# Layer 2's experts in a four-layer hybrid: gate logits moved into the attention's steps, networks computed four at a time

## The chip, the core and the metric

The program runs on one core of one Trainium2 chip, in one launch. Its time is device microseconds (us) of that core; the kernel before has a median of 11329.03 us over 3 runs (11311.37 to 11329.67).

The engines are TensorE (PE; its weight loads are listed as PEld), VectorE (DVE), ScalarE (ACT), GpSimd (POOL) and SyncE (SP). Every transfer in this program is issued on SP, in the order of one queue. All arithmetic is in 32-bit floats.

## The reference, cut to what matters

Four layers work on x of shape 4 x 64 x 64 x 128 (4 images, 4096 tokens of 128 channels). Layer 2 is an attention followed by the experts that the change touches:

```
t = t + attention(ln(t))
t = t + experts(ln(t))

def experts(x):                                    # x: 4 images x 4096 tokens x 128
    logits = einsum('bsd,ed->bse', x, gate_w) + gate_b      # 64 experts
    probs  = softmax(logits, axis=1)                        # over the 4096 tokens
    topv, topi = the 8 highest of each image and expert
    pooled = sum over the 8 of topv * x[topi]               # 4 x 64 x 128
    h   = gelu([pooled, 1] @ weight1)                       # 129 -> 512, one network an expert
    out = [h, 1] @ weight2                                  # 513 -> 128
    each of the 8 tokens gets topv * out added
```

The weights are 64 networks of 129 x 512 and 513 x 128 floats, some 33.7 MB, and each network is applied to just 4 vectors (one an image).

## The kernel before, in words

The layers run one after another. Layers 0 and 1 and layer 2's attention are interleaved in hand-written generators; `experts` and the start of `layer3` are plain code whose order on each engine is chosen by a planner (it keeps the order of the code unless an instruction would have to wait for something longer than a later one).

**The attention** (`recurrence_and_attention`) walks a list `seq` of 4 images x 8 query blocks of 512 tokens x 16 steps (512 steps). A step issues, in this order, the scores of the step two ahead (`scores(g + 2)`: two matmuls L1351 and their exponentials L1355), a second exponential (L1394), and the two matmuls of its own pair of key tiles into `avs` (L1399). The order on PE, ACT and DVE is exactly the order of the code there (`manual_schedule`); SP and POOL are ordered by the planner. Between these, two generators are advanced: `own` prepares the next image (`prepare`, with `unit` for layer 1's recurrence; several advances a step, none while the last image is worked on), and `side`, advanced once a step, does the block's small work: `finish` of the block before (normalise, add the residual in the tile `tb`, store it to `xa` at L1319) and `query` of the block after. A `yield` in a generator is the place where it hands back to the step. `finish` and `query` share one PSUM bank, `blk`.

**The experts** (`experts`) then load all of `xa` into a resident tile `t` (32 transfers, L2059). Images are taken in pairs, one image's 64 experts on partitions 0 to 63 and the other's on 64 to 127. For a pair: layer norm into `xl` (L135, L137, L85, L142), transposes (L103), logits (L1449, evacuated by ACT at L1450) into `wt`; softmax and the choice of the 8 highest over 4096 columns (L1455 to L1465, one long instruction each); transposes of the weights (L103) and the pooled sums (L1476), with the tokens as the stationary operand.

The networks follow, two experts a turn (`EG = 2`). The *weights* are the stationary operand: 8 matmuls of 128 x 128 with a moving operand of 4 columns for the first layer (L1502), bias (L1507), Gelu (L1512), 8 more for the second (L1516). A 32-bit matmul is two records in the trace, so a turn has 16 records of each. The weights are loaded in a ring of 3 (L1490, L1495). At the end the outputs are laid out as `oute` (L1525, L1529), and for each of 32 blocks 4 matmuls (L1537) form the scattered sum, which DVE adds to `t` (L1542) and SP stores to `x2` (L1543). Layer 3 loads `x2` again (L1659).

Buffers come from stacked pools. A pool that lies where an earlier one lay starts only when every tile of the earlier one has been released.

Of the kernel before, what the change touches and what calls it, by code (L numbers as in the profile page):

```python
# [14 lines left out]
P = 128  # L15
B = 4
# [27 lines left out]
EG = 2  # L44
# [834 lines left out]
def recurrence_and_attention(cm, x1, W, V, sp_d, x2, last):  # L879
# [7 lines left out]
    with ExitStack() as ctx:  # L887
# [17 lines left out]
        nc.vector.memset(qrow[:, P - 1 : P], -0.5)  # L905
        with tc.tile_pool(name="rwp", bufs=2) as lp, tc.tile_pool(
# [30 lines left out]
            nc.vector.tensor_copy(wv[:, D : D + 1], cm.ident[:, P - 1 : P])  # L937

# [357 lines left out]
        def finish(b, k):  # L1296
# [23 lines left out]
            yield  # L1320

# [16 lines left out]

        NP = NT // 2
        seq = [(b, k, p) for b in range(B) for k in range(NBLK) for p in range(NP)]  # L1340
        avs, res, es = {}, {}, {}
# [23 lines left out]
        with tc.manual_schedule(engines=engines):  # L1365
# [4 lines left out]
            for g, (b, k, p) in enumerate(seq):  # L1370
                if k == 0 and p == 0:
                    own = prepare(b + 1, own_bank) if b + 1 < B else iter(())
                if p == 0:
                    gens = []
                    if g:
                        gens.append(finish(*seq[g - 1][0:2]))
                    if k + 1 < NBLK:
                        gens.append(query(b, k + 1, block_bank))
                    side = steps(*gens)
                    tb = tl(p2, [P, 4, D], "tb")  # L1380
                    nc.sync.dma_start(tb, rows(img[b]["t"], 0, k))
                    res[b, k] = tb
                    avs[b, k] = tl(avp, [P, BLK], "av")
                if p == NP - 3:
                    for _ in side:
                        pass
                    if k == NBLK - 1:
                        for _ in own:
                            pass
# [16 lines left out]
            for _ in finish(*seq[-1][0:2]):  # L1406
                pass
# [3 lines left out]
def experts(cm, W, t, x2):  # L1411
    tc, nc = cm.tc, cm.nc
    with ExitStack() as ctx:
        wp = ctx.enter_context(tc.tile_pool(name="xw", bufs=1))
        wl = ctx.enter_context(tc.tile_pool(name="xwl", bufs=3))
        mm = ctx.enter_context(tc.tile_pool(name="xmm", bufs=6, space=PSUM))
        acc = ctx.enter_context(tc.tile_pool(name="xacc", bufs=2, space=PSUM))

        gwT = tl(wp, [P, E2], "gwT")
        b1T = tl(wp, [P, H2 // P, E2], "b1T")  # L1420
        with tc.tile_pool(name="xwp", bufs=2) as lp:
            cm.load_transposed(gwT, W["gate_w"], lp, mm, "mm")
            for c in range(H2 // P):
                cm.load_transposed(
                    b1T[:, c, :], W["weight1"][:, D, c * P : (c + 1) * P], lp, mm, "mm"
                )
        gb = tl(wp, [P, 1], "gb")
        b2 = tl(wp, [P, D], "b2")
        with nc.allow_non_contiguous_dma(reason="a bias laid over partitions"):
            for i in range(2):  # L1430
                half = slice(i * E2, (i + 1) * E2)
                nc.sync.dma_start(gb[half, :], W["gate_b"].unsqueeze(1))
                nc.sync.dma_start(b2[half, :], W["weight2"][:, H2, :])
# [3 lines left out]
        pooled = tl(wp, [P, E2, B], "pooled")  # L1437
        with tc.tile_pool(name="xb", bufs=1) as bp, tc.tile_pool(name="x2", bufs=2) as p2:
            for pr in range(2):
                xl = tl(bp, [P, 2, NT, D], "xl")  # L1440
                lg = wt[:, pr, :]
                for i in range(2):
                    cm.layer_norm(xl[:, i], t[:, 2 * pr + i], p2)
                    half = slice(i * E2, (i + 1) * E2)
                    for k in range(NBLK):
                        xT = tl(p2, [P, BLK], "xT")
                        cm.transpose4(xT, xl[:, i, 4 * k : 4 * k + 4, :], mm, "mm", act=False)
                        ps = tl(mm, [P, BLK], "mm")
                        nc.tensor.matmul(ps[half, :], lhsT=gwT, rhs=xT, start=True, stop=True)  # L1449
                        nc.scalar.activation(  # L1450
                            lg[half, k * BLK : (k + 1) * BLK], ps[half, :], AF.Identity,
                            bias=gb[half, :],
                        )
# [12 lines left out]
                wT = tl(bp, [P, NT, P], "wT")  # L1466
                for k in range(NBLK):
                    cm.transpose4(
                        wT[:, 4 * k : 4 * k + 4, :].rearrange("p a c -> p (a c)"),
                        lg[:, k * BLK : (k + 1) * BLK].rearrange("p (a c) -> p a c", c=P),  # L1470
                        mm, "mm", act=(k % 2 == 0),
                    )
                for i in range(2):
                    ps = tl(acc, [P, BLK], "acc")
                    for k in range(NT):
                        nc.tensor.matmul(  # L1476
                            ps[:, 0:E2], lhsT=xl[:, i, k, :],
                            rhs=wT[:, k, i * E2 : (i + 1) * E2],
                            start=(k == 0), stop=(k == NT - 1),
                        )  # L1480
                    nc.vector.tensor_copy(pooled[:, :, 2 * pr + i], ps[:, 0:E2])


        NC2 = H2 // P
        outT = tl(wp, [P, B, E2], "outT")
        oute = tl(wp, [P, 2, D], "oute")
        with tc.tile_pool(name="xh", bufs=3) as hp:
            for e0 in range(0, E2, EG):
                w1 = tl(wl, [P, EG, H2], "w1")
                nc.sync.dma_start(  # L1490
                    w1, W["weight1"][e0 : e0 + EG, 0:D, :].rearrange("e d h -> d e h")
                )
                w2 = tl(wl, [P, EG, NC2, D], "w2")
                for j in range(EG):
                    nc.sync.dma_start(  # L1495
                        w2[:, j],
                        W["weight2"][e0 + j, 0:H2, :].rearrange("(c p) o -> p c o", p=P),
                    )
                ph = tl(mm, [P, NC2, EG, B], "mm")
                for j in range(EG):  # L1500
                    for c in range(NC2):
                        nc.tensor.matmul(  # L1502
                            ph[:, c, j, :], lhsT=w1[:, j, c * P : (c + 1) * P],
                            rhs=pooled[:, e0 + j, :], start=True, stop=True,
                        )
                hh = tl(hp, [P, NC2, EG, B], "hh")
                nc.vector.tensor_tensor(  # L1507
                    hh, ph,
                    b1T[:, :, e0 : e0 + EG].unsqueeze(3).to_broadcast([P, NC2, EG, B]),
                    ALU.add,  # L1510
                )
                nc.scalar.activation(hh, hh, AF.Gelu)  # L1512
                po = tl(acc, [P, EG, B], "acc")
                for j in range(EG):
                    for c in range(NC2):
                        nc.tensor.matmul(  # L1516
                            po[:, j, :], lhsT=w2[:, j, c, :], rhs=hh[:, c, j, :],
                            start=(c == 0), stop=(c == NC2 - 1),
                        )
                nc.vector.tensor_copy(  # L1520
                    outT[:, :, e0 : e0 + EG], po.rearrange("p e b -> p b e")
                )
        for pr in range(2):
            ps = tl(mm, [P, BLK], "mm")
            nc.tensor.transpose(  # L1525
                ps[:, 0:P], outT[:, 2 * pr : 2 * pr + 2, :].rearrange("p b e -> p (b e)"),
                cm.ident,
            )
            nc.vector.tensor_tensor(oute[:, pr, :], ps[:, 0:P], b2, ALU.add)  # L1529
# [594 lines left out]
```

## Time and profile before

| what | value |
|---|---|
| median of 3 runs (lowest, highest) | 11329.03 us (11311.37, 11329.67) |
| the profiled execution: time, span in the trace | 11343.32 us, 11341.5 us |
| mean granted TensorE clock | 0.881 |
| busy share of the span: PE, DVE, ACT, POOL | 85%, 68%, 46%, 48% |
| attention's steps: first and last L1351 or L1399 | 6793.2 to 8811.5 us |
| experts: from there to the issue of the last store to `x2` (L1543) | to 9349.98 us |
| layer 3's first products (L1716) | 9404.65 us |

The attention's steps and the experts are 2018 us and 538 us of the span. The page's shares are means over stages of very different kinds, so the views used below are cut to stretches of these two. A row of the table by stretch gives the stretch, its length, busy us and number of instructions of each engine, the granted clock, the mean busy share of the 16 DMA engines (this can pass 1) and GB/s. A row of the groups gives line, engine, operation, output and inputs, shape, count, busy us and mean ns of one, then the engine's idle time before such an instruction and who ended it.

### The profile page before, as it was taken

The numbers are of one execution on the slowest core, as the hardware profiler recorded it, in microseconds if no ns is written. First come the engines' busy times: TensorE is split into PE (matmuls) and PEld (weight loads), VectorE is DVE, ScalarE is ACT, GpSimd is POOL, SyncE is SP. The second block draws the span as 40 slices with busy tenths as digits, with TensorE's granted clock in tenths as the row PEclk, the third lists the DMA queues.
The fourth block names the chain that finished last, engine by engine and source line by source line (L and its number), as shares of the span: only waits on it lengthen the run. The fifth ranks groups of instructions, "written<-read, shape, count | busy, mean of one in ns | idle before, by whom it ended". The sixth has DMA issues, their size and how long they took to land. (4 is left out here: it accounts for less than half of the span.)

```text
span 11341.5 us, 163279 instructions
## 1 busy us (share of the span) xinstructions
PE 9650.1 (85%) x59692; PEld 4750.2 (42%) x59692; DVE 7675.5 (68%) x11366; ACT 5226.4 (46%) x13141; POOL 5433.6 (48%) x2629
## 2 busy tenths in 40 slices
PE   6889998889997899988899739999999598687685
PEld 2344443344443344433444324444444394444442
DVE  1898898888988889888999775354410413565563
ACT  6666444555445564445522127677766102132230
POOL 0788888888888888888899610000000000110110
PEclk7899999899998899998999869999999755688785
DMA  5334443334443344433333321110000141000100
GB/s 146 107 110 147 129 126 116 114 113 151 139 128 116 110 140 139 136 121 113 105 109 101 127 65 31 32 33 28 22 12 9 48 140 14 6 15 10 14 8 8
DMA packets 1338551, 946.41 MB, mean 83 GB/s; under 512 B 692421, under 2 KB 1159849, under 8 KB 1333657
## 3 DMA queue, kind: packets, MB, share of 16 engines
q1 hardware_dynamic: 1337752, 935.95, 27.5%
q8 instruction: 478, 7.83, 0.3%
q14 instruction: 321, 2.62, 0.1%
HBM read 633.46 MB, written 302.12 MB: 82 GB/s over the span
## 5 line engine op out<-in xcount | busy, mean ns | idle before, releaser
L657 DVE TENSOR_TENSOR_SCAN big<-dA,db 128x1024 f32<-128x1024 f32 x2048 | 4679.9, 2286 | 81.1 <-ACT dA L564 2.8
L673 POOL TENSOR_TENSOR big<-big,ct 128x2048 f32<-128x2048 f32 x1024 | 4646.5, 4538 | 85.5 <-DVE big L657 6.1
L641 PE MATMUL db<-dg,du 64*64 64x512 f32 x16384 | 2446.6, 618 | 100.6 <-DVE db L654 87.6
L686 PE MATMUL aux<-big,both 128*64 128x256 f32 x16384 | 2109.8, 401 | 471.6 <-DVE db L654 257.1
L686 PEld LDWEIGHTS aux<-big,both 128*64 128x64 f32 x16384 | 1203.2, 142 | 1466.0 <-issue 625.9
L705 ACT COPY yr<-aux 128x64 f32<-128x64 f32 x1024 | 226.2, 221 | 2758.8 <-PE aux L686 1315.2
L641 PEld LDWEIGHTS db<-dg,du 64*64 64x64 f32 x16384 | 747.7, 136 | 1323.7 <-issue 1220.5
L612 ACT ACTIVATE dg<-mask,BT 128x64 f32<-128x64 f32 x4096 | 1007.3, 341 | 5.9 <-DMA dg_d<-dg 5.9
L1399 PE MATMUL av<-e,x 128*128 128x512 f32 x2048 | 974.0, 592 | 5.9 <-ACT e L1394 5.9
L1351 PE MATMUL qk<-a,xT 128*128 128x512 f32 x2048 | 963.3, 593 | 9.8 <-ACT e L1355 9.0
L1355 ACT ACTIVATE e<-qk,nk 128x512 f32<-128x512 f32 x1024 | 692.3, 685 | 539.6 <-PE qk L1351 538.8
L564 ACT ACTIVATE dA<-dp,A 128x252 f32<-128x252 f32 x2048 | 870.6, 509 | 1.4
L1809 POOL COPY vp<-vt 72x160 f32<-72x160 f32 x56 | 19.0, 345 | 1389.9 <-PE po L1815 1082.0
L968 POOL TENSOR_TENSOR ln_rs<-ln_rs,qrow 128x8 f32<-128x8 f32 x16 | 26.2, 1640 | 1323.7 <-DVE ln_rs L967 1323.7
L665 POOL TENSOR_TENSOR cy<-big,a 128x32 f32<-128x32 f32 x1008 | 271.2, 269 | 742.5 <-DVE big L657 480.0
L1351 PEld LDWEIGHTS qk<-a,xT 128*128 128x128 f32 x2048 | 383.0, 190 | 467.9 <-issue 371.3
L1399 PEld LDWEIGHTS av<-e,x 128*128 128x128 f32 x2048 | 381.6, 190 | 436.1 <-issue 394.4
L2009 DVE SCALAR_TENSOR_TENSOR t<-x,gw,t 128x128 f32<-128x128 f32 x1024 | 354.2, 346 | 302.8 <-PE x L2003 279.8
L1394 ACT ACTIVATE e<-e 128x1024 f32<-128x1024 f32 x510 | 538.7, 1056 | 15.5
L1634 POOL MEMSET f<- 128x2016 f32 x1 | 1.8, 1778 | 1093.1 <-DMA t<-x 1093.1
L654 DVE TENSOR_TENSOR db<-db,cy 128x16 f32<-128x16 f32 x2016 | 336.2, 167 | 262.6 <-PE db L641 210.7
L1799 ACT ACTIVATE e<-s 72x576 f32<-72x576 f32 x448 | 269.8, 643 | 513.6 <-PE s L1792 513.1
(482 smaller groups left out, 11417.8 us busy)
## 6 DMA issues: line engine op xcount, KB each, us to landing
ct<-ct_d SPq DMA_DIRECT2D x1024, 128.0 KB
dg_d<-dg SPq DMA_DIRECT2D x256, 512.0 KB
dg<-dg_d SPq DMA_DIRECT2D x256, 512.0 KB
xo<-xT_d SPq DMA_DIRECT2D x2048, 32.0 KB
x<-xc_d SPq DMA_DIRECT2D x144, 264.0 KB
dp<-dl_d SPq DMA_DIRECT2D x256, 128.0 KB
t2k<-in_x SPq DMA_DIRECT2D x96, 256.0 KB
sp<-sp_d SPq DMA_DIRECT2D x16, 1280.0 KB
```

The costliest lines, as they stand in the source:

```text
L564: nc.scalar.activation(w["dA"][:, :, g, n, 1:], w["dp"][:, g, :, 1:], AF.Exp, scale=A[:, w["h"], g, n : n + 1],)
L612: nc.scalar.activation(q["dg"][:, n, :], mask, AF.Copy, scale=BT[:, q["c"], n : n + 1])
L641: nc.tensor.matmul(bs[j][p * TC : (p + 1) * TC, g * NH0 : (g + 1) * NH0, :], lhsT=q["du"][kp][half, g * TC : (g + 1) * TC], rhs=q["dg"][ha ...
L654: nc.vector.tensor_tensor(bs[j][:, :, 0], bs[j][:, :, 0], old[:, u, :], ALU.add)
L657: nc.vector.tensor_tensor_scan(st[:, u].rearrange("p n t -> p (n t)"), q["w"]["dA"][:, c % QC].rearrange("p g n t -> p (g n t)"), bs[j].re ...
L673: nc.gpsimd.tensor_tensor(sv, sv, q["ct"].rearrange("p n t -> p (n t)").unsqueeze(1) .to_broadcast([P, 4, NH0 * TC]), ALU.mult,)
L686: nc.tensor.matmul(yp[p * TC : (p + 1) * TC], lhsT=both, rhs=st[:, :, p * NH0 + n, :], start=(n == 0), stop=(n == NH0 - 1 and not late),)
L1351: nc.tensor.matmul(ps, lhsT=me["xT"][:, kt * P : (kt + 1) * P], rhs=me["a"][k], start=True, stop=True,)
L1355: nc.scalar.activation(e[:, j, :], ps, AF.Exp, bias=me["nk"][:, kt : kt + 1], scale=2.0)
L1394: nc.scalar.activation(es[g + 2], es[g + 2], AF.Exp)
L1399: nc.tensor.matmul(avs[b, k], lhsT=img[b]["x"][:, kt, :], rhs=e[:, j, :], start=(kt == 0), stop=(kt == NT - 1),)
L2009: nc.vector.scalar_tensor_tensor(t[:, j, :], s[:, e, :], gw[:, j, 4 * a + e : 4 * a + e + 1], t[:, j, :], ALU.mult, ALU.add,)
```

## The change

1. **Logits in the attention's steps.** A new generator `gate(b, k)` runs in `side`, behind `finish` and `query`: layer norm of the finished block `tb` (the root by POOL), a store of the normalised tokens `xh` to `xh_d`, four transposes, a copy, one matmul with `gwT`, bias by ACT, and a store of the logits to `lg_d`. The forced end of `side` moves from three steps before a block's end to the next block's start. Two small loads (`gb`) and one transposed load (`gwT`) move to the attention's set-up.
2. **No resident tokens.** `experts` loads the logits (two transfers of 2 MB) and, block by block, `xh` for the pooled sums and `xa` for the residual at the end (a ring of 6). The pooled sums have the tokens as the moving operand, on two halves of the columns.
3. **The networks.** Four experts a turn. `pooled` is widened from 4 to 32 columns by zeros. The *weights* move: four matmuls of 512 columns with 32 stationary columns, each on its own quarter of the columns, then bias and Gelu on a 128 x 512 tile, four transposes, and 16 matmuls of 128 moving columns, again on quarters. Biases of the first layer come as four loads of one row each, repeated over 32 partitions. The outputs go to DRAM in four small stores a turn and are read back as `oute`.
4. **Loads ahead.** The ring holds 5 turns (20 experts); its first 5 loads stand ahead of everything but the logits' loads.

```diff
-EG = 2
+EG = 4
 # recurrence_and_attention, set-up
+        gwT = tl(wp, [P, E2], "gwT")
+        gb = tl(wp, [P, 1], "gb")
...
+            cm.load_transposed(gwT, G["gate_w"], lp, pp, "mm")
+        def gate(b, k):
+            tb = done.pop((b, k))
...
+            for i in range(4):
+                nc.vector.bn_stats(st[:, i, :], tb[:, i, :])
+            for i in range(4):
+                nc.vector.bn_aggr(mv[:, i, :], st[:, i, :])
+            inverse_root(rs, mv[:, :, 1])
+            yield
+            yield
+            xh = tl(p3, [P, 4, D], "xh")
+            for i in range(4):
+                nc.vector.tensor_scalar(
+                    xh[:, i, :], tb[:, i, :], mv[:, i, 0:1], rs[:, i : i + 1],
+                    ALU.subtract, ALU.mult,
+                )
+            nc.sync.dma_start(rows(xh_d, b, k), xh)
+            yield
+            yield
+            ps = block_bank()
+            turned(ps, xh)
+            xhT = tl(p3, [P, BLK], "xhT")
+            nc.vector.tensor_copy(xhT, ps)
+            yield
+            yield
+            half = slice(b % 2 * E2, (b % 2 + 1) * E2)
+            ps = block_bank()
+            nc.tensor.matmul(ps[half, :], lhsT=gwT, rhs=xhT, start=True, stop=True)
+            lg = tl(p3, [P, BLK], "lg")
+            nc.scalar.activation(lg[half, :], ps[half, :], AF.Identity, bias=gb[half, :])
+            nc.sync.dma_start(lg_d[half, b // 2, k * BLK : (k + 1) * BLK], lg[half, :])
+            yield
 # the loop over the steps, at a block's first step
+                    for _ in side:
+                        pass
                     gens = []
                     if g:
                         gens.append(finish(*seq[g - 1][0:2]))
                     if k + 1 < NBLK:
                         gens.append(query(b, k + 1, block_bank))
+                    if g:
+                        gens.append(gate(*seq[g - 1][0:2]))
...
-            for _ in finish(*seq[-1][0:2]):
+            for _ in steps(finish(*seq[-1][0:2]), gate(*seq[-1][0:2])):
 # experts
+        wl = ctx.enter_context(tc.tile_pool(name="xwl", bufs=5))
         wp = ctx.enter_context(tc.tile_pool(name="xw", bufs=1))
-        wl = ctx.enter_context(tc.tile_pool(name="xwl", bufs=3))
...
+        for pr in range(2):
+            nc.sync.dma_start(wt[:, pr, :], lg_d[:, pr, :])
...
+        def weights(e0):
+            w1 = tl(wl, [P, EG, H2], "w1")
+            nc.sync.dma_start(
+                w1, W["weight1"][e0 : e0 + EG, 0:D, :].rearrange("e d h -> d e h")
+            )
...
+            for j in range(EG):
+                nc.sync.dma_start(
+                    w2[:, j], W["weight2"][e0 + j, 0:H2, :].rearrange("(c p) o -> p c o", p=P)
+                )
+                nc.sync.dma_start(
+                    b1[32 * j : 32 * j + 32, :],
+                    W["weight1"][e0 + j, D : D + 1, :].to_broadcast([32, H2]),
+                )
+            return w1, w2, b1
+        AHEAD = 5
+        ready = [weights(e0) for e0 in range(0, AHEAD * EG, EG)]
 # pooled sums, per pair and block
+                    for j in range(4):
+                        for i in range(2):
+                            half = slice(i * E2, (i + 1) * E2)
+                            nc.tensor.matmul(
+                                po[half, 0:D], lhsT=wT[:, j, half], rhs=xs[i][:, j, :],
+                                start=(4 * k + j == 0), stop=(4 * k + j == NT - 1),
+                            )
 # networks, per turn
+                w1, w2, b1 = ready.pop(0)
+                ph = tl(mm, [P, H2], "mm")
                 for j in range(EG):
+                    nc.tensor.matmul(
+                        ph[32 * j : 32 * j + 32, :], lhsT=pooled[:, e0 + j, :], rhs=w1[:, j, :],
+                        start=True, stop=True,
+                    )
...
+                nc.vector.tensor_tensor(flat, ph, b1, ALU.add)
+                nc.scalar.activation(flat, flat, AF.Gelu)
...
+                cm.transpose4(hT.rearrange("p c h -> p (c h)"), hh, mm, "mm", act=False)
...
+                for c in range(NC2):
+                    for j in range(EG):
+                        col = slice(32 * j, 32 * j + 32)
                         nc.tensor.matmul(
+                            po[col, 0:D], lhsT=hT[:, c, col], rhs=w2[:, j, c, :],
                             start=(c == 0), stop=(c == NC2 - 1),
                         )
...
+                if e0 + AHEAD * EG < E2:
+                    ready.append(weights(e0 + AHEAD * EG))
...
+                for b in range(B):
+                    nc.sync.dma_start(oe_d[b, e0 : e0 + EG, :], so[b::32, :])
```

## The prediction

> **What bounds the kernel now.** I read the page first for the span (11341.5 us, one execution of 11343.3; the runs shown have a median of 11329.0, so I sum a difference against the profiled execution and take it from the median). Then the busy times by stretch around the change:
>
> ```profile
> 8594.70:8811.80 217.10, 217.10 (x531) 97.97 (x529) 10.39 (x30) 145.41 (x181) 0.00 (x0) 1.00 0.03 9
> 8811.80:8856.20 44.40, 3.32 (x14) 1.87 (x13) 33.26 (x207) 1.93 (x3) 0.00 (x0) 0.54 0.93 235
> 8856.20:8908.80 52.60, 30.78 (x96) 11.26 (x96) 32.18 (x146) 11.45 (x18) 0.00 (x0) 0.81 0.11 31
> 8908.80:8933.30 24.50, 0.03 (x1) 0.06 (x1) 20.28 (x7) 5.09 (x4) 0.00 (x0) 0.54 0.00 0
> 8933.30:8953.80 20.50, 20.20 (x160) 20.06 (x160) 3.31 (x7) 2.34 (x4) 0.00 (x0) 0.89 0.00 1
> 8953.80:9056.50 102.70, 56.05 (x256) 32.52 (x256) 50.82 (x94) 18.36 (x23) 0.00 (x0) 0.72 0.00 0
> 9056.50:9296.30 239.80, 222.76 (x1026) 219.91 (x1026) 11.84 (x66) 7.33 (x32) 0.00 (x0) 0.50 0.43 127
> 9296.30:9350.00 53.70, 52.92 (x256) 52.62 (x256) 26.18 (x59) 1.88 (x3) 0.00 (x0) 0.50 0.61 171
> ```
>
> Row 1 is the last image's attention: PE is busy for the whole of it. Rows 2 to 6 are loads and layer norm, logits, softmax and pooled sums of pair 0, then pair 1: 245 us in which no engine is full. Row 7 is the networks, with PE and its weight loads full at clock 0.50 and the DMA engines under half. Row 8 is the scattered sum. The chain of waits has only PE in rows 7 and 8; the DMA's best rates stand in narrower stretches:
>
> ```profile
> 9094.01 3.57 PE acc L1516 x16
> 9097.58 3.43 PE mm L1502 x16
> ...
> 9296.30 52.93 PE mm L1537 x256
> ```
>
> ```profile
> 8825.00:8830.00 5.00, 0.00 (x0) 0.00 (x0) 4.98 (x42) 1.21 (x1) 0.00 (x0) 0.50 1.22 290
> ...
> 8855.00:8860.00 5.00, 1.52 (x5) 0.91 (x5) 4.04 (x16) 0.00 (x0) 0.00 (x0) 0.50 1.07 342
> ```
>
> The first is the 512-byte rows of `t<-xa`, the second mostly 2 KB rows of `weight1`.
>
> **1. Gate in the attention.** PE is full there, so its work is paid at its streaming time. Two records of 512 columns take 0.86 us (four take 1.72 in the chain). Four transposes take 0.43 at full clock (weight loads of L103 at 8877.96: 0.42). So 1.29 us a block, 31 blocks: **+40 us**. Upper bound by whole rows with their latency (0.66 and 1.04): 53. Lower bound: 40, nothing hides it. DVE gets 4 statistics (0.87), 4 scalings (1.3) and a copy (0.69), ACT 0.68, POOL one root (L968, 0.55 to 1.64) a block; DVE is 36% and ACT 70% busy over 6790 to 8815, so these cost nothing unless late. The new waits: DVE waits for POOL's root (behind it all of `own`'s DVE work), PE waits for `xh` and `xhT` (behind it the scores, and ACT's exponentials for those). Two yields, 6.9 us, stand between each. Images 0 to 2 have blocks of 58 to 69 us against 58.4 in the last, so there a late DVE may cost up to 1 us more a block: 0 to +24, I take 0. The stores (256 and 128 KB a block) pass SP's `tb`, `xt` and `sp` loads at a DMA share of 0.08. The forced end of `side` moves, but `query` ends at step 8 of 16 and is needed at 14. The gate's set-up (one more transpose, loads of `gwT` and `gb`) passes through SP and DVE beside layer 0's end: 0 to 2, I take 0.
>
> **2. After the last step (8811.5 = 0).** Rows 2, 3 and most of 6 go. What comes:
>
> Last `finish` and gate, now unhidden: `tb` at +4.7 (8816.2); statistics 1.5, root 1.6, scaling 1.3: +9.3; transposes 1.2, copy 0.7, matmul 2.0, bias 0.7: +14; store landed at +17 (3.1 as from a load's issue at 8815.38 to its reader at 8818.51).
>
> Loads can't start earlier: the ring of weights lies over the attention's pools, `rw` with `wv` and now `gwT` among them, and the trace shows such a wait:
>
> ```profile
> 8812.21 0.52 SPq L1432 DMA_DIRECT2D gb<-in_L_ffn_gate_b  x1
> ...
> 8815.38 0.92 SPq L2059 DMA_DIRECT2D t<-xa  x2
> 8816.40 0.45 SPq L1319 DMA_DIRECT2D xa<-tb  x1
> ```
>
> SP was idle, yet `t`, which lies over `rw`, was loaded only after `wv`'s last reader. So nothing is ahead of the attention's end: logits of pair 0 and three blocks of `xh` from +9.3, weights from +14.
>
> Softmax: 24.5 a pair (row 4), pair 0 from about +17 to +42, pair 1 to about +66. The DMA engines are slower than that: logits 4.2 MB, five turns of weights (w1 1.05, w2 1.05, repeated bias 0.26: 2.36 MB) 11.8, `xh` 8.4, together 24.4 MB at 300 GB/s = 81 us, from +10 to **+91**. I take 300, near the 290 of like rows; ends are 342 and row 2's mean of 235, which costs 63 over this, the turns and the scatter: 11162. `xh` stands behind the weights on SP, so the pooled sums end with the last load, some 5 later: +96.
>
> Networks, PE of a turn. The trace has 32-column quarters in layer 0's convolution:
>
> ```profile
> 1048.92 2.78 PE L370 MATMUL bg<-x,cdiag 96*32 96x512 f32 x24
> ```
>
> 24 records of 512 columns in 2.78 us, where one alone costs 0.43: four run side by side. So 1.7 + 0.9 + 1.7 us a turn at half clock (layers, transposes), 4.3 against 14.0 now (2 x 7.0, for the same four experts). DVE 1.7, ACT 0.7. The DMA needs 2.36 MB / 300 = 7.9, and SP 13 issues x 0.37 to 0.6 = 5 to 8. So **the loads bound it**. First ring free at +96 + 8.5 = +104.5; 11 turns x 7.9 = 87: +191.5; last turn's way through the engines 8 (4.3 + 1.7 + 0.7 and handovers): +199.5. Outputs to DRAM and back, 2 x 3: +205.5.
>
> The trace's loads hide each other's latency: 30 loads of `t` were issued in 26.95 us, 0.9 each, their data's time at 290. By that row the 64 bias loads cost their bytes alone, as summed. The Trainium skill, "DMA: Bandwidth & Descriptors", Rules for kernel authors, says against it that transfers below 64 KB are mostly overhead, and these are at that size; with the 0.6 us to the first byte of its Specifications paid in full 64 times, an estimate is 38 us more.
>
> The convolution's row shows quarters beside each other, but no change between them and full-width work inside a turn. The Trainium skill, "TensorEngine Tiling (Array Packing)", Key Properties, says that a change of tiling mode drains TensorE, and a turn makes two each way; the sum would stay as it is while the drains are below a turn's 3.6 us of slack on PE, and no run here shows them.
>
> Scattered sum: PE as before 53 (L1537, bound by its weight loads). The DMA now also loads `xa`: 8.4 + 8.4 MB, and 2.1 of layer 3's loads, at 300: 63. With a ring of 6, SP holds a load until a store has landed, and stores queue behind it: 53 to 75, I take 63: **+268.5**. Layer 3's first norm must now wait for the last store (its scratch lies over the ring of `xa`), its parameters no longer do: 0 +- 5.
>
> **Sum.** Experts 538.5 now, 268.5 then: -270; attention +40: **-230**. 11343.3 - 230 = 11113 for the profiled execution, 11329 - 230 = **11099** by the median.
>
> **Rivals.**
> - *Faster loads* (5%): at 340 GB/s with part of the ring in flight before the end, the 81 becomes 55, the 87 becomes 77, the scatter 55: 44 more, 11055. For: the 342 row. Against: it lasts 5 us, and `xa` has 512-byte rows.
> - *Small loads bind* (12%): if a bias load ran on one of 16 engines (300/16 = 19 GB/s, 64 KB = 3.5 us), a turn would take 14 instead of 7.9: 16 x 6.1 = 98 less: 11197. No row has such a load in number.
> - *Quarters don't overlap across different weights* (5%): a turn is 6.9 + 0.9 + 6.9 = 14.7 on PE, 16 turns 235 where I have 103: 11231. Against: the 2.78 row has different weights too.
> - *The change does not do what it says in the attention, slower* (4%): the gate's chain DVE, POOL, DVE, PE comes late in a crowded image, PE waits at the transposes, and the scores behind it with it. Every us counts there. It decides from 270/31 = 8.7 us a block in all, 7.4 beyond the gate's own 1.29, two steps late. At four steps (13.7) in 24 blocks: +330 - 230 = +100: 11429. For: blocks up to 69 us show that PE waits sometimes. Against: DVE's waits for POOL are 1.8 us each (L1259).
> - *The same mechanism, one handover of two steps late* (3%): 6.9 + 1.3 a block ends within 0.2% of now.
>
> **Numbers.** Forecast 71%, own range 11050 to 11140 (loads 290 to 340, attention +40 to +64, scatter 53 to 75). To hold 8 in 10 I reach to most of the small loads' case: 11050 to 11200. Faster by over 0.2% (23 us, about what a measurement of this kernel can tell from no change): 71 + 5 + 12 + 5 = 93; within: 3; slower: 4.
>
> **What would show it.** Right: a block of the last image at 59.7 us where it is 58.4; no weights before the last gate; DMA share near 1 from +10 to +190 but for a gap before turn 5; turns of 7 to 9 us on PE with gaps ended by DMA; L1537's successor at 53 to 75. Wrong: blocks over 62 us with PE waiting for `xh`; turns of 14 us; loads of weights inside the attention; the scatter at over 80 with SP waiting for stores.

## The result, and the profile after

The changed kernel takes 11155.2 us (median of 4 runs, 11136.7 to 11161.6) where before takes 11328.2 beside it (4 runs): a ratio of 0.9848, 95% interval 0.9831 to 0.9865, some 173 us less where 230 were forecast. The profiled execution of after has a span of 11159.9 us, of the 11161.6 that this execution took; that of before is 11341.5, so the two differ by 181.6.

Where the time went is read from six points that both traces have: the last scan of layer 0, the first scores, the end of the last `av`, the scatter's first matmul and last addition, and layer 3's first product. Between them lie, in us:

| stretch | before | after | difference |
|---|---|---|---|
| start to layer 0's last scan | 6390.1 | 6408.3 | +18.2 |
| to the first scores (set-up) | 403.1 | 407.4 | +4.3 |
| attention, to the end of the last `av` | 2019.0 | 2067.8 | +48.8 |
| experts, to the scatter's first matmul | 484.2 | 216.5 | -267.7 |
| scatter, to its last addition | 53.6 | 57.1 | +3.5 |
| to layer 3's first product | 54.7 | 73.3 | +18.6 |
| to the end | 1936.9 | 1929.4 | -7.5 |

The five middle rows, which the change touches, make -192.5. The first and the last are runs of the same instructions: in the traces of all fourteen kernels, the last scan ends between 6390 and 6434 us, and layer 3 takes 1893 to 1937 from its first product. Before's scan is the earliest of the fourteen; whether the change has any share in the +18.2 can't be told from single traces. The middle rows repeat far better: nine kernels with after's attention have 2067.8 or 2067.9; four with after's experts have 215.8 to 219.9; nine with after's order at layer 3's start have 73.0 to 76.5. So the experiments are read by stretches. A stretch is still read from one trace of each kernel, and the 4 us between those four traces with the same experts are its margin.

After, by stretches (from, to, length, then busy us and instructions of PE, weight loads, DVE, ACT and POOL, PE's granted clock, DMA share, GB/s):

```profile
8660.00:8870.00 210.00, 210.00 (x522) 94.28 (x521) 22.52 (x86) 140.44 (x175) 4.02 (x4) 1.00 0.06 16
```
```profile
8883.50:8900.00 16.50, 5.06 (x15) 2.47 (x14) 6.95 (x23) 0.68 (x1) 1.01 (x1) 0.58 0.49 169
8900.00:8944.00 44.00, 6.21 (x32) 6.01 (x32) 39.91 (x14) 8.77 (x6) 0.00 (x0) 0.54 1.09 310
8944.00:8982.00 38.00, 27.55 (x290) 21.57 (x290) 0.76 (x3) 9.23 (x17) 0.00 (x0) 0.87 0.84 230
8982.00:9002.00 20.00, 13.94 (x146) 6.01 (x146) 6.34 (x11) 3.10 (x5) 0.00 (x0) 0.91 0.75 223
9002.00:9080.00 78.00, 44.58 (x491) 23.06 (x494) 17.38 (x33) 6.92 (x11) 0.00 (x0) 0.72 0.94 262
9100.00:9157.10 57.10, 52.91 (x256) 52.61 (x256) 22.27 (x33) 0.00 (x0) 0.00 (x0) 0.50 1.01 286
```

The first row answers to the last image of before: PE is still busy for all of it, and a block has grown from 58.40 to 60.04 us. The next rows are the stretch in which before had no full engine and then a full PE. Now the DMA engines are full beside the softmax, at 310 GB/s; they move 230 while the tokens come for the pooled sums, and 262 in the networks, where PE is busy for 44.6 of 78 us. In the chain of waits, the networks are now transfers, and SP's issues of them, where before they were PE. A piece of that chain, from 9040 to 9062:

```profile
by line: DMA w<-in_L_ffn_weight 84.6%; SPq L1486 8.5%; SPq L1483 7.2%; issue 2.3%; SPq L1477 1.8%
...
9041.40 7.75 DMA w<-in_L_ffn_weight
```

The step from attention to experts on SP's queue (start, duration, line, transfer):

```profile
8897.26 0.45 SPq L1361 DMA_DIRECT2D lg_d<-lg  x1
8897.76 1.24 SPq L1473 DMA_DIRECT2D b<-in_L_ffn_weight  x2
8899.10 0.52 SPq L1477 DMA_DIRECT2D w<-in_L_ffn_weight  x1
8900.30 0.33 SPq L1470 DMA_DIRECT2D wt<-lg_d  x1
```

The first weights are asked for 15.6 us after the last `av` (8883.5), behind the gate of the last block; none is loaded inside the attention.

### The profile page after: what moved, and what is told of

Read it like the earlier page. It is cut to its first block, busy times and chain, and to the rows that moved or that the text cites. A ratio compares the mean times of both kernels' runs of the same rounds, so it can differ in the third digit from the quotient of the medians.

```text
span 11159.9 us, 163057 instructions
## 1 busy us (share of the span) xinstructions
PE 9472.5 (85%) x59368; PEld 4541.5 (41%) x59368; DVE 7705.4 (69%) x11365; ACT 5228.1 (47%) x13128; POOL 5468.6 (49%) x2661
## 5 line engine op out<-in xcount | busy, mean ns | idle before, releaser
L641 PE MATMUL db<-dg,du 64*64 64x512 f32 x16384 | 2449.2, 619 | 100.5 <-DVE db L654 87.6
L973 POOL TENSOR_TENSOR g_rs<-g_rs,qrow 128x4 f32<-128x4 f32 x32 | 41.1, 1285 | 1500.4 <-DVE g_rs L972 1500.4
L2058 PE MATMUL x<-ew,x3T 128*128 128x512 f32 x512 | 365.0, 802 | 158.6 <-DVE t L2064 153.6
```

Source lines behind the costliest of these rows:

```text
L641: nc.tensor.matmul(bs[j][p * TC : (p + 1) * TC, g * NH0 : (g + 1) * NH0, :], lhsT=q["du"][kp][half, g * TC : (g + 1) * TC], rhs=q["dg"][ha ...
L2058: nc.tensor.matmul(s.rearrange("p e c -> p (e c)"), lhsT=x3T[:, j * P : (j + 1) * P], rhs=ew[:, 4 * a : 4 * a + 4, :].rearrange("p e c -> ...
```

## The experiments

Each kernel is after with one edit, unless it says otherwise; line numbers in the views are those of the kernel shown. "Stretch" is the time from the end of the last `av` to the scatter's first matmul, 216.5 us in after (215.8 to 219.9 in the four traces with these experts). A "turn" of the networks is the time from one Gelu to the next once their weights are no longer there beforehand, 9.0 us in after. The theories and rivals are those of the text quoted ahead of each result. Where no ratio is given, the kernel ran once, and its whole time says little: without the transposes, for instance, it is 11172.8 us, more than after with less work.

### The price of the gate

**The gate alone.** Before, with after's attention; the experts are before's own. (`experts` and `EG` as before; `gate`, `gwT`, `gb`, `xh_d`, `lg_d` as after.)

> The kernel before, with part 1 of the change alone: the gate runs in the attention's steps and stores its logits and normed tokens to DRAM, where nothing reads them; the experts compute their own as before. Forecast's theory (the gate costs its streaming time, 1.29 us a block): +40 us, a last-image block of 59.7 us. What the trace after shows (60.04 against 58.40 in the last image, +49 over the 31 blocks; the rest of the lead lost elsewhere): +49 us and a last-image block of 60.0. Rival (the gate's set-up also delays what comes before the first scores, since in the trace after they start 22.5 us later, of which 18.2 arose before layer 0's last scan): +70. The last scan's time in this run's profile, whose instructions up to there are those of before, shows whether the 18.2 us belong to the change at all: if they are the scatter of single executions, it will stand anywhere between 6388 and 6406.

Ratio 1.0056 (1.0039 to 1.0073), so +44 to +83 us. Its attention takes 2067.9, its last-image blocks 60.04, its set-up 406.8, its last scan ends at 6402.0; its experts take 478.2 up to the scatter, where before has 484.2. So part 1 is +48.9 and about +4, not +40, and none of that is lost in the experts. The ratio alone would not tell +49 from +70; the trace does, since the set-up is 4 us longer and the last scan stands elsewhere again.

**Without the transposes**, so that the logits mean nothing:

```
-            ps = block_bank()
-            turned(ps, xh)
-            nc.vector.tensor_copy(xhT, ps)
+            nc.vector.tensor_copy(xhT, xh.rearrange("p i c -> p (i c)"))
```

> After, with the gate's four transposes a block left out on PE (its logits are then taken of tokens that were not turned, and mean nothing); statistics, scaling, copy, matmul, bias and stores are all still there. After's block costs 1.64 us more than before's in the last image. Theory A (PE is paid at its streaming time): 0.43 less a block, 59.6 in the last image, 13 us less over the 31 blocks. Theory B (each change between kinds of matmul on PE costs the start of one, so a group costs its whole span): 0.60 to 0.66 less a block, 59.4, 19 us less over all.

A last-image block takes 59.60: 0.44 less, where theory A said 0.43. Over the 31 blocks it is 7.6 us and not 13: in the first three images most blocks are shorter by 0.4 us too, some by 0 to 0.25, and two are 1.65 us longer. So the transposes were priced rightly where PE is full throughout, and the 0.34 us a block above the forecast sit elsewhere. After's PE in the last image shows where (start, duration; a group's price is the distance to the next start):

```profile
8864.56 0.60 PE L968 MATMUL blk<-ident,xh 128*128 128x128 f32 x4
8865.00 1.88 PE L1394 MATMUL qk<-a,xT 128*128 128x512 f32 x4
8866.71 1.88 PE L1443 MATMUL av<-e,x 128*128 128x512 f32 x4
8868.43 1.88 PE L1394 MATMUL qk<-a,xT 128*128 128x512 f32 x4
8870.15 1.88 PE L1443 MATMUL av<-e,x 128*128 128x512 f32 x4
8871.96 1.07 PE L1358 MATMUL blk<-xhT,gwT 128*64 128x512 f32 x2
8872.96 1.98 PE L1394 MATMUL qk<-a,xT 128*128 128x512 f32 x4
8874.78 1.45 PE L1443 MATMUL av<-e,x 128*128 128x512 f32 x3
```

The transposes cost 0.44. A group of four costs 1.71 or 1.72 among its like, but 1.81 ahead of the 64-column gate and 1.82 behind it, and the gate itself 1.00 for 0.86.

**The gate 128 columns wide:**

```
-        gwT = tl(wp, [P, E2], "gwT")
+        gwT = tl(wp, [P, 2, E2], "gwT")
...
+            nc.vector.tensor_copy(gwT[:, 1, :], gwT[:, 0, :])
...
-            nc.tensor.matmul(ps[half, :], lhsT=gwT, rhs=xhT, start=True, stop=True)
+            nc.tensor.matmul(
+                ps, lhsT=gwT.rearrange("p i e -> p (i e)"), rhs=xhT, start=True, stop=True
+            )
```

> After, with the gate's weights laid twice side by side, so that its matmul is 128 x 128 like its neighbours on PE and not 128 x 64 (half of its output is not read). In after's trace the gate's group of two records stands 1.00 us from its start to the next group's, where groups of that length take 0.86, and the groups ahead of it and behind it take 1.81 and 1.82 for 1.72 and 1.71: 0.34 us a block beyond the streaming time. Theory A (the change of shape on PE costs it, to 64 columns and back): a block of the last image takes 59.70 us, the forecast's, where after has 60.04; the 31 blocks 5 to 11 us less. Rival (it is the wait for a bank, or for the copy): 60.04 stays.

```profile
8860.52 1.88 PE L1446 MATMUL av<-e,x 128*128 128x512 f32 x4
8862.23 1.02 PE L1359 MATMUL blk<-xhT,gwT 128*128 128x512 f32 x2
8863.09 1.45 PE L1397 MATMUL qk<-a,xT 128*128 128x512 f32 x3
```

The steps are 1.71 and 0.86, and a block takes 59.70, the forecast's number. The attention is 6.7 us shorter (in the last kernel below, which has this gate too, 8.3). Theory A: what costs is that the gate's matmul has another shape than its neighbours.

### What sets the networks' turn

**The old networks in the new frame** (weights standing, four columns moving, 32 matmuls or 64 records a turn; the outputs are turned back by two transposes, with no stores to DRAM, and the biases added are not the right ones). An excerpt of the edit:

```
+                            ph[:, c, j, :], lhsT=w1[:, j, c * P : (c + 1) * P],
+                            rhs=pooled[:, e0 + j, 0:B], start=True, stop=True,
```

> After, with the networks computed as before inside the new frame: the weights stand, the four pooled columns of an expert move, 128 matmuls a turn, the outputs turned back by two transposes; gate, loads ahead, repeated biases and scattered sum are after's. (The bias added is a wrong one of the same size.) Theory A (moving weights on four quarters is what took PE out of the way): a turn is bound by PE at the 14.0 us of before, 16 turns 224, so from the attention's end to the scattered sum 98 + 224 + 2 = 324 us where after has 216.5; the whole +105 to +110 against after. Rival (the gain of the networks came from the loads that stand ready, not from the form of the matmuls): turns stay at 9 and the stretch within 10 us of after.

Stretch 324.5, whole 11255.5 (one run), turns of 14.5 us. The networks are PE's again:

```profile
8995.00:9195.00 200.00, 193.38 (x900) 192.51 (x900) 5.54 (x28) 3.33 (x13) 0.00 (x0) 0.50 0.44 125
```

So 108 of the 268 us come from the form of the matmuls, given the rest of the new frame, and the other 160 from that rest. The form may be worth some us more, since this kernel also lacks after's 64 small stores.

**One turn's biases for all** (the other 15 turns' biases are left out):

```
+                if e0 == 0:
                     nc.sync.dma_start(
                         b1[32 * j : 32 * j + 32, :],
                         W["weight1"][e0 + j, D : D + 1, :].to_broadcast([32, H2]),
                     )
```

> After, but the repeated biases of the first layer are loaded for the first turn alone and used in all 16 (the other turns' biases are left out): 60 of 64 loads of 64 KB go, 9 loads and stores-to-issue a turn less 4 of 13. Theory A (the loads bound the networks by their bytes): a turn moves 2.10 MB and not 2.36, so 9.0 us become 8.0, and the first five turns' loads end 3.5 us earlier: 11 x 1.0 + 3.5 = 14 us less than after. Theory B (the number of transfers bounds it: SP's issue, or a fixed price of each): 9/13 of 9.0 = 6.2 us a turn, so 31 us less in the 11 turns, and more in the first five: 35 to 45 us less than after. Theory C (another wait sets the turn): 9.0 stays.

Stretch 193.1, 23.4 less: between A (14) and B (35 to 45). Turns of 6.8 us, 303 GB/s:

```profile
9005.00:9070.00 65.00, 40.45 (x489) 20.29 (x487) 17.86 (x32) 7.55 (x12) 0.00 (x0) 0.81 1.05 303
```

So 60 loads of 64 KB cost 0.39 us each, where the forecast's 300 GB/s make 0.22. The margin of 4 us makes 0.07 a load.

**As many transfers, without the repetition** (the kernel just shown, and four 2 KB rows a turn that nobody reads; biases as there):

```
+                else:
+                    nc.sync.dma_start(
+                        row[32 * j : 32 * j + 1, :], W["weight1"][e0 + j, D : D + 1, :]
+                    )
```

> The kernel with one turn's biases again (turns of 6.8 us), plus four transfers a turn that each load one row of 2 KB of the biases, read by nobody: after's number of transfers, without the 32-fold repetition of their bytes. (The biases used are the first turn's, as there.) Theory A (the price of the bias loads lies in their repeated bytes: 60 loads of 64 KB took 23.4 us, 0.39 each, where 64 KB at 300 GB/s are 0.22): turns stay at 6.8 to 7.0 and the stretch from the attention's end to the scattered sum at 193 to 196. Theory B (a fixed price of each transfer, whatever its size): turns go back to 8.5 to 9.0, the stretch to 210 to 216.

Stretch 200.8: 7.7 back of 23.4, turns of 7.2 us. By these two traces A has about two thirds and B one: 0.13 us for each transfer as such, 0.26 for its 64 KB, each within 0.07. In the networks the DMA engines have less to do here, not more:

```profile
8990.00:9050.00 60.00, 37.80 (x400) 19.26 (x400) 14.27 (x27) 6.29 (x10) 0.00 (x0) 0.69 0.88 248
```

So the price of a small transfer as such does not show as busy time in the mean over the 16 engines (the trace does not tell them apart).

**Outputs stored last** (64 stores of 2 KB become 4 of 32 KB):

```
-                    nc.sync.dma_start(oe_d[b, e0 : e0 + EG, :], so[b::32, :])
+        for b in range(B):
+            nc.sync.dma_start(oe_d[b].rearrange("(t j) o -> j t o", j=EG), so[b::32])
```

> After, but the experts' outputs are gathered in SBUF and stored by 4 transfers behind the last turn where after has 64 of 2 KB between the loads. Theory A (the small stores are what holds the loads at 262 GB/s in the networks, where 310 was had before them): turns of 9.0 fall to 7.6, 15 us less. Rival (the repeated biases are what holds the loads down, as turns of 6.8 us at 303 GB/s without them say; the stores only share SP): turns stay at 9.0, and the stretch from the attention's end to the scattered sum stays within 4 us of after's 216.5.

The rival falls. Stretch 204.2, 12.3 less: turns of 8.0, 301 GB/s:

```profile
9002.00:9070.00 68.00, 43.65 (x445) 19.61 (x446) 17.53 (x32) 6.93 (x11) 0.00 (x0) 0.82 1.11 301
```

The 60 stores that went cost 0.2 us each, though they carry 2 KB. Of the 12.3 us, 9.7 are an earlier end of the networks, and 2.6 a shorter way from there to the scatter (6.0 us for 8.5), since in after the last stores stand ahead of the loads of `oute`. Both kinds of small transfer hold the loads down: the DMA engines' busy share is 0.94 with the stores and 1.11 without. By what way is not shown. SP issues 113 transfers in after's row of 78 us and its issues stand in the chain above; and in 9002 to 9092 DVE's addition ahead of the Gelu waits 21.5 us, in four places, for what the profile names as a landing store. No run separates the two.

**A ring of 3:**

```
-        wl = ctx.enter_context(tc.tile_pool(name="xwl", bufs=5))
+        wl = ctx.enter_context(tc.tile_pool(name="xwl", bufs=3))
-        AHEAD = 5
+        AHEAD = 3
```

> After with a ring of 3 turns of weights where it has 5. Theory A (the DMA engines' bytes bound the stretch; how far ahead weights stand only shifts which bytes come first): pooled sums end 15 us earlier (4.7 MB less stand ahead of the tokens), the turns that find their weights ready are 3 and not 5, and the stretch from the attention's end to the scattered sum is 205 to 220 us as in after (216.5). Rival (the loads ahead are what hides the loads' latency): turns of 10 to 12 us, the stretch 230 to 250.

Stretch 211.8; the first Gelu comes 80.8 us after the attention's end where after has 100.5; turns of 7 to 10. Theory A: a ring of 3 loses nothing. The edit also did something that was not expected of it: the load of pair 0's logits is issued 0.2 us after the attention's end and not 8.7, so the 4.7 us less may come from that, and a small worth of the depth could hide behind it.

**Tokens' loads earlier** (`tokens` makes the 16 loads of a pair, into 8 buffers for each image of it):

```
+            for pr in range(2):
+                early = [tokens(pr, k) for k in range(NBLK)]
+                for e0 in (range(0, 2 * EG, EG), range(2 * EG, AHEAD * EG, EG))[pr]:
+                    ready.append(weights(e0))
```

> After, with the loads of the normed tokens moved ahead on SP: pair 0's before the second and later loads of weights, pair 1's behind two turns of weights where they stood behind all five; 8 buffers for each where there were 3. Bytes and instructions are the same. Theory A (the DMA engines' bytes bound everything from the attention's end to the networks' end, and only the stretch in which they are not full is lost, 39 us at 231 GB/s and 20 us at 223 where 300 is had): pooled sums end near +72 instead of +98, turns keep 9 us while the queue is full, and the networks end 8 to 14 us earlier than after. Theory B (what counts is when the pooled sums end, as in the forecast's sum, where the ring's first free buffer follows them): 25 us earlier. Theory C (the order moves nothing): within 3 us of after.

First Gelu at +78.2, 22 us earlier; stretch 207.1, 9.4 less, where theory A said 8 to 14 and B 25. What is gained is time in which the DMA engines were not full, and the sums' earlier end itself is not. Ratio 0.9836 (0.9819 to 0.9852), which can't be told from after's.

### Layer 3's start

In before, image 0's tokens (`t<-x`) were asked for among the scatter's stores, the last three loads right behind the last store, and most of the parameters only then:

```profile
9350.39 1.79 SPq L1659 DMA_DIRECT2D t<-x  x3
9353.35 0.35 SPq L1572 DMA_DIRECT2D bdn<-in_L_attn_b_down  x1
```

After, on SP, behind the last stores of the scatter, most of the parameters come first:

```profile
9157.14 0.36 SPq L1598 DMA_DIRECT2D x<-t  x1
9157.55 0.49 SPq L1639 DMA_DIRECT2D wo<-in_L_attn_out_proj_w  x1
...
9178.61 0.33 SPq L1707 DMA_DIRECT2D io<-in_iota  x1
9178.99 13.47 SPq L1714 DMA_DIRECT2D t<-x  x16
```

**Image 0 first** (its 8 loads written at the head of `layer3`):

```
+        first = image(0)
         wdT = tl(wp, [P, DK], "wdT")
...
+            t = image(b) if b else first
```

> After, with layer 3's loads of image 0 written ahead of its parameters' loads, so that they stand right behind the last store of x2 on SP. Theory A (in after, layer 3 starts late because image 0's 8 loads stand behind some 40 parameter loads on SP, which were issued from 9158 to 9179): the time from the last store to layer 3's first product falls from 73 us to 52 to 58, the whole by 15 to 21 us. Rival (the parameters set the start themselves, being late now where they were loaded during the scattered sum before): within 5 us of after.

```profile
9179.43 0.36 SPq L1598 DMA_DIRECT2D x<-t  x1
9179.84 5.69 SPq L1627 DMA_DIRECT2D t<-x  x7
9185.63 0.87 SPq L93 DMA_DIRECT2D lt_in<-in_L_attn_w_down  x1
```

57.5 us to the first product where after has 73.3, and before 54.7: theory A, for 15.8 of the 18.6 us. The whole time's ratio, 0.9827 (0.9810 to 0.9843), can't show 16 us.

### A version with all of it

The wide gate, the tokens' loads earlier and image 0 first, and two new edits: the biases as a 4 x 512 tile that a matmul adds, and the outputs placed by one-hot matmuls (by a matrix of zeros and ones), with no stores.

```
+                nc.tensor.matmul(ph, lhsT=sel, rhs=b1, start=True, stop=False)
...
+                    nc.tensor.matmul(
+                        out2[b // 2][half, 0:D], lhsT=hot[:, b, E2 - EG - e0 : 2 * E2 - EG - e0],
+                        rhs=so, start=(e0 == 0), stop=(e0 == E2 - EG),
+                    )
```

> After with everything that the runs so far point to. Tokens' loads early; layer 3's image 0 ahead of its parameters; the gate's matmul 128 columns wide; one load of 8 KB for a turn's four bias rows, which a matmul with a 4 x 128 selector lays over the quarters in PSUM (no repeated rows, no addition on DVE); the outputs put in their places by four one-hot matmuls a turn that sum in PSUM, with no transfer to DRAM and back. Theory A (bytes at 300 to 310 GB/s from +11 us on, 46 MB, and a last turn of 6 us): 165 to 175 us from the attention's end to the scattered sum, where after has 216.5; layer 3's start 16 less, attention 5 to 11 less: 62 to 75 us less than after, a ratio of 0.977 to 0.979 to before. Rival (each of the gains is of the same idle time, so that they don't add): 190 to 205 in the stretch, 30 to 45 us less than after.

11097.2 (5 runs), ratio 0.9783 (0.9768 to 0.9798); stretch 194.0, where theory A said 165 to 175 and the rival 190 to 205. The rival has the number and not the reason, for the loads are done early, as in A. What A had wrong is the end:

```profile
9000.00:9030.00 30.00, 21.75 (x258) 10.38 (x252) 4.62 (x9) 2.98 (x5) 0.00 (x0) 0.95 1.12 332
9030.00:9066.00 36.00, 29.40 (x188) 11.97 (x180) 3.24 (x7) 1.93 (x4) 0.00 (x0) 0.50 0.09 21
```

The loads run at 332 GB/s and are done some 152 us after the attention's end. Then four turns of 10.0 us follow at a granted clock of 0.50, in which PE waits for ACT and DVE at each step of the one turn under way, 2.0 us a turn by these rows (the text quoted next says 3):

```profile
9050.74 1.12 PE L1594 MATMUL out<-so,hot 128*64 128x128 f32 x8 [0.41 <-DVE so L1591]
9051.79 2.07 PE L1569 MATMUL mm<-b,sel 4*128 4x512 f32 x2
9053.79 1.94 PE L1571 MATMUL mm<-w,pooled 128*32 128x512 f32 x8
9056.50 1.12 PE L103 MATMUL mm<-ident,hh 128*128 128x128 f32 x4 [0.78 <-ACT hh L1577]
9058.40 1.94 PE L1584 MATMUL acc<-w,hT 128*32 128x128 f32 x32 [0.78 <-DVE hT L107]
```

**Turns laid over one another** (order on PE: transposes of turn n-1, first layer of n, second layer of n-1, one-hot of n-2, written out by hand):

> The version with all the gains together, with the networks' turns laid over one another: the first layer of a turn stands on PE between the transposes and the second layer of the turn before, and the one-hot matmuls come a turn later. In that version the loads are done at +151 us from the attention's end, but four turns of 10.0 us at a granted clock of 0.50 still follow, in which PE stands idle 3 us a turn, since each turn runs through PE, ACT, PE, DVE, PE, DVE and PE by itself. Theory A (this chain, not the loads, is what the stretch of 194 us ends with): turns follow the loads (6.4 to 7.0 us), two turns of 8 us of PE's own work remain behind the last load, and the stretch falls to 165 to 172 us, the whole 22 to 29 us below that version, a ratio of 0.975 to 0.977 to before. Rival (PE itself, at the low clock, is the bound by now: about 8 us a turn): 178 to 188 in the stretch, 6 to 16 us less.

11059.7 (5 runs, 11051.6 to 11070.9) where before has 11323.3; ratio 0.9772 (0.9758 to 0.9785), which overlaps the last kernel's. Stretch 164.1, 30 less: theory A, just below its 165 to 172. The rows from the stretch's second part to the scatter:

```profile
8935.00:8975.00 40.00, 38.40 (x439) 19.49 (x439) 8.85 (x18) 6.76 (x11) 0.00 (x0) 0.91 1.10 323
8975.00:9008.00 33.00, 26.73 (x270) 13.45 (x270) 4.38 (x11) 2.98 (x5) 0.00 (x0) 0.79 1.11 325
9008.00:9024.50 16.50, 13.56 (x157) 7.47 (x157) 3.94 (x9) 1.20 (x2) 1.72 (x2) 0.79 0.60 170
```

The DMA engines are full until some 16 us before the scatter, and no row of DMA idleness like that of 9030 to 9066 is left. The granted clock of the last two rows is 0.79 where it was 0.50, so the filled waits and the higher clock come together in these 30 us and are not told apart. From the first scores to layer 3's first product this trace has 2339.8 us, the kernel before it 2372.7, after 2414.7, before 2611.5.

## Why the prediction was right, and where it fell short

The direction, the mechanism and most of the sum held: -192.5 by the stretches where -230 was summed. The number held less well: 11155 lies outside the forecast's own range, 11050 to 11140, and inside the wider one, 11050 to 11200, which had been opened for a case that did not come in the form described (small loads that each run on one engine). What carried the time there is in good part layer 3's start (18.6 us, where 5 were allowed) and the parts that the change does not touch, so that the wide range holds is partly luck. By its steps:

- **Gate, +40: +48.8, and +4.3 of set-up (406.8 to 408.0 in most later traces, 400 to 404 in three; before 403.1: not settled).** "So 1.29 us a block" failed by a term that it lacked: the 64-column matmul among 128-column ones costs 0.34 us a block more than its streaming time (59.70 with the wide gate, 60.04 without), 6.7 to 8.3 us over the attention. The prediction weighed such a change of shape for the networks alone, where PE had slack, and not here, where it had none. The late DVE, taken as 0, cost nothing on average: the blocks of images 0 to 2 (55.8 to 69.5 us in the trace of before, not 58 to 69) grew by 1.5 to 1.6 us, no more than the last image's 1.64, though single ones grew by 0.4 to 2.8.
- **Loads not before the attention's end, weights at +14, pooled sums +96:** +15.6 us for the first weights, +98.6 for the first matmul of the networks. Right, and so was the gap in the DMA's share before the ring is refilled (0.84 and 0.75 in the rows of 8944 to 9002).
- **"The loads bound it", at 7.9 us a turn:** right in kind (PE busy 44.6 of 78 us; 14.5-us turns with the old networks), 9.0 in size. The 300 GB/s failed: 262, since the 64 stores of 2 KB were not priced among the loads at all (0.2 us each) and the biases cost 0.39 each where "their bytes alone" make 0.22. The loads of the last eleven turns took some 102 us (first issue at 8983.3, last bytes at 9085) where 87 were summed. Part of that came back: they began at +99.7 and not at +104.5, because a buffer came free as soon as its first matmuls were done, and the last turn took 6.5 and not 8. Networks 109.3 against 103.5.
- **Outputs 2 x 3 us:** 8.5, from the end of PE's last matmul (9091.5) to the scatter's first. The last 24 small stores hold SP until 9095.7, and the loads of `oute` stand behind them.
- **Scatter 63:** 57.1 at 286 GB/s. The 2.1 MB of layer 3's loads that were summed here were all issued behind it.
- **Layer 3's start, 0 +- 5: +18.6.** This step failed. It asked which loads would have to wait, found that the parameters no longer would, and did not ask what they would stand in front of: image 0's tokens, on the same queue. Four of the parameters' loads went before or during the scatter; the others were issued behind its last store, from 9157.6 to 9178.9, and held the tokens for 21 us. With the tokens written first, 15.8 of the 18.6 us are gone.

13.1 for the gate and its set-up, 5.8 for experts and scatter and 18.6 for layer 3 are the 37.5 us between -230 and -192.5. In the two profiled executions the parts that the change does not touch give +10.7, which makes the -181.6 of the spans. The 8.6 us from there to the -173 of the medians lie in executions without a trace.

Of the rivals, *small loads bind* had the direction: small transfers made turns of 9.0 us, not of 14, and a bias load cost 0.39 us, not 3.5. *Quarters don't overlap* is excluded by PE's busy time, *late gate* by blocks that grew by 1.5 to 1.6 us where it needed 8.7, *faster loads* by the first weights at +15.6 and 310 GB/s at best over 44 us.

Two pages can now be set against runs. The Trainium skill, "TensorEngine Tiling (Array Packing)", Key Properties, says that a change of tiling mode drains TensorE. The 0.34 us for the change to 64 columns and back, where PE is full, fit this; no trace shows the drain itself. The Trainium skill, "DMA: Bandwidth & Descriptors", Rules for kernel authors, says that transfers under 64 KB are mostly overhead. The 2 KB stores agree with it, at 0.2 us each. The 64 KB loads cost about 0.13 as transfers and 0.26 as bytes, so at that size the bytes are still the greater part. The estimate of 38 us more that the prediction gave by that page was too much: 60 of the loads cost 23.4 in all, 10 more than their bytes at 300 GB/s.

## What to carry to other kernels

When a stage becomes bound by its transfers, price every transfer, the smallest too: the repeated biases cost 23.4 us here and 60 stores of 2 KB 12.3, and matmuls with a 4-row selector and a one-hot table did their work on PE, which had room while the loads ran. When a wait goes, ask what will now be issued ahead of whom on the queue, not only what can start. Work put into a stage whose PE is full is worth trying in the shape of its neighbours. A stage rid of its transfers must then be looked at for the chain inside one turn.

## What the runs showed of the hardware

- A 128 x 64 matmul of 512 columns among 128 x 128 ones took 1.00 us where a 128 x 128 one takes 0.86, and made the groups before and after it 0.09 and 0.10 longer.
- With 64 stores of 2 KB and 64 repeated loads of 64 KB among the large loads, the DMA engines moved 262 GB/s; without the stores 301, without the repeated loads 303, without both (in versions with other edits too) 323 to 332.
- In the version with all of it, the last turns of the networks ran at a granted clock of 0.50 with PE busy for 29.4 of 36 us, though it was 0.95 in the 30 us before.
